# Convolutions one turn further ahead, in one stretch with the gate and the lora products

## The chip, the cores and the metric

The kernel runs on one core of a Trainium2 chip, as one launch. The metric is the device time of that core in microseconds (us). A number of runs is taken of each kernel and the median is compared; one more execution is recorded by the hardware profiler, and that is where the lines of this document come from.

## The reference

128 samples of 64 channels by 1024 positions pass through two residual layers, all in float32.

```
h   = gelu(cond @ W0 + b0); h = gelu(h @ W1 + b1)
att = softmax(h @ W2 + b2)                       # 8 weights per sample
y0  = (att-mixed 64x64 matrix of the sample) @ x + att @ bias_k
x   = x + (y0 @ B) @ A.T + ffn_bias              # rank 128, layer 0
y   = grouped conv(x, 9 taps, 4 groups) + context(cond) + fside
x   = x + y @ W_up.T + lora(y)                   # layer 1, W_up 1024 x 1024
lora(y): one of 4 experts by argmax(y @ gate_w.T + expert_bias), rank 8
```

## The kernel before

Two samples of 64 channels make a *pair* of 128 rows by 1024 columns; there are 64 pairs. Layer 1 works on two pairs at a time, so the main loop has 32 turns, d = 0 to 31. `manual_schedule` makes each engine run its instructions in the order in which the program emits them, and the order is written out by hand; nothing is reordered by a planner. A tile is handed on when its last reader is done, and tiles of one tag rotate through a fixed number of buffers. The tag "bank" has 4 PSUM banks, used in turn by almost everything; pb0 to pb3 are 4 further banks for the layer 1 products. x has 8 buffers, xt 3, yt 2, the convolution's input X 3.

*Layer 0 of a pair* is `layer0_in` (xt times B, L330, then a copy on ScalarE), `layer0_mix` (the mixing matrix, L340, then z on VectorE, or on ScalarE for the first four pairs) and `layer0_out` (z times AT, L361; VectorE adds it to x, L362). `layer0_out` then writes x to a DRAM tile x1d and reads it back in another arrangement as X, both from SyncE's DMA queue (L363, L368, L369). The mixing matrices of the first four pairs are built on the core (`own_bd`); those of the others are computed for all samples at once by `agg_all`, written to DRAM (`agg_out`) and read back in groups of two pairs by `load_cond`, with their bias rows (`load_rows`, "ab") and context rows ("cx").

*The convolution of a pair* has 9 taps over columns that are interleaved, so that even and odd columns share part of the work. `shared_in` multiplies X by the summed taps (L400), `shared_out` adds the context on VectorE (L415) and copies halves across partitions on ScalarE (L418). `differences` makes differences of neighbouring columns on GpSimd (L392, L393). `conv_in` multiplies those by the taps (L438), once for each sample, and `conv_out` adds the shared part on VectorE (L450), which gives y in the tile yt. Pairs 0 and 1 use a plain form (L429). The matmuls of L400, L429, L438 and of the gate (L496) use 64 of the array's columns each and go by twos to the two halves of the output's partitions; the profile shows them as 128\*64. Those of lora (L573) use 32 rows each and go by fours (32\*128). All others are 128\*128.

*Layer 1 of two pairs* multiplies 256 rows of y by W_up by a scheme with seven half-size products instead of eight: `ffn_sums` makes four sums of y on GpSimd (s0 to s3, L485 to L488), and `w_sum` makes combinations of W_up's quarters once at the start (T1, T2, T3, -T4 from w11, w12, w21, w22, on VectorE). `ffn_a` is the first product (and ScalarE's copy v of it, L479); `ffn` holds the others (all L465), u2 and u3 on VectorE (L556, L560), their adds to x on GpSimd (L561 to L563), the gate (`gate_in` L496, a copy zg on ScalarE, `gate` L511 and a chain of small VectorE instructions), the turn of the masked lora inputs (L536), the four lora products (L573) and the final adds to x on VectorE (L575), after which SyncE writes the two pairs out.

In turn d, TensorE does: the second product of d; gate and shared sum of pair 2d+2; T2, gate's fold, T3, T1, the last two products; lora; taps of 2d+2 and shared sum of 2d+3; layer 0 in of pairs 2d+4 and 2d+5; taps of 2d+3; the rest of layer 0 around the first product of d+1. Pairs are so convolved in the turn before they are used. GpSimd's queue holds, in a turn: the four sums, differences, two adds of the layer 0 bias (`add_fbias`, L581), the u adds, differences, and the loads of two pairs (`load_x`, xt L108 and x L109), where each load waits for a free buffer.

Of the kernel before, what the change touches and what calls it, by code (L numbers as in the profile page):

```python
# [41 lines left out]
P = 128  # L42
# [15 lines left out]
N = 512  # L58
# [10 lines left out]
def block(ctx: ExitStack, tc: tile.TileContext, a: dict, out: bass.AP):  # L69
# [65 lines left out]
        eng.dma_start(W[name], a[f"w{name}"])  # L135

    def load_w12(eng):
        for h in range(2):
            W12.append(tmp.tile([P, HC // 2, N], F32, tag=f"tmp{h}", name=f"w12_{h}"))
            eng.dma_start(W12[h], a["w12"][:, h * HC // 2 : (h + 1) * HC // 2])  # L140

    def w_sum(name, x, y):
        W[name] = const.tile([P, HC, N], F32, name=f"w{name}")
        if "12" not in (x, y):
            nc.vector.tensor_tensor(W[name], W[x], W[y], ALU.subtract)
            return
        for h in range(2):
            part = slice(h * HC // 2, (h + 1) * HC // 2)
            u, w = (W12[h] if n == "12" else W[n][:, part] for n in (x, y))
            nc.vector.tensor_tensor(W[name][:, part], u, w, ALU.subtract)  # L150


    X = []
# [24 lines left out]
    def load_cond(g):  # L178

        if g * GP >= FIRST:  # L180
            bds[g] = BD[g % NBD]
            for b in range(2):
                nc.sync.dma_start(
                    bds[g].rearrange("(r two) t b o -> two r t b o", two=2)[b, :, :, b, :],
                    aggd.rearrange("(t two) r o -> two r t o", two=2)[b, :, g * GP : (g + 1) * GP],
                )
            load_rows(g, aggbs, aggbd, "ab")
        load_rows(g, ctxs, ctxd, "cx")

    def load_rows(g, tiles, src, tag):  # L190
# [107 lines left out]

    def agg_all():

        first = ytp.tile([NB, 4, 512], F32, tag="yt", name="agg0")
        second = [xpool.tile([NB, 2, 512], F32, tag="x", name=f"agg1{j}") for j in range(2)]
        to = aggd.rearrange("b i o -> b (i o)").rearrange("b (j h n) -> h b j n", j=4, h=2)
        aggs.extend([(to[0], first), (to[1][:, :2], second[0]), (to[1][:, 2:], second[1])])
        for h in range(2):
            ps4 = [spare(j, f"pagg{h}_{j}") for j in range(4)]
            for j in range(4):
                rows = slice(32 * j, 32 * (j + 1))
                nc.tensor.matmul(ps4[j], attT[rows, :], wa[rows, h], start=True, stop=True)
            for j in range(4):  # L310
                to = second[j // 2][:, j % 2] if h else first[:, j]
                if j % 2:
                    nc.scalar.copy(to, ps4[j])
                else:
                    nc.vector.tensor_copy(to, ps4[j])
            yield

    def agg_out():
# [1 line left out]
            nc.sync.dma_start(to, agg)  # L320


    xbs, z0s, yts, opened = {}, {}, {}, {}
    diffs, pms, m2s, pcs = {}, {}, {}, {}

    def layer0_in(pr):
        xt = xts.pop(pr)
# [146 lines left out]
    def ffn_a(d):  # L474

        opened[d] = [psb.tile([P, N], F32, tag=f"pb{i}", name=f"pb{i}_{d}") for i in range(4)]
        product(opened[d][0], halves(d)[0][0], W["11"])
        v = sums.tile([P, N], F32, tag="v", name=f"v{d}")
        nc.scalar.copy(v, opened[d][0])  # L479
        return v  # L480

    def ffn_sums(d):
        (a0, a1), (b0, b1) = halves(d)
        s = [sums.tile([P, HC, P], F32, tag=f"s{i}", name=f"s{i}_{d}") for i in range(4)]
        nc.gpsimd.tensor_tensor(s[0], b0, b1, ALU.add)  # L485
        nc.gpsimd.tensor_tensor(s[1], s[0], a0, ALU.subtract)  # L486
        nc.gpsimd.tensor_tensor(s[2], a0, b0, ALU.subtract)
        nc.gpsimd.tensor_tensor(s[3], a1, s[1], ALU.subtract)  # L488
        return s

    def gate_in(d):
        yt = yts[d]
        pg = bank(f"pg{d}")
        for c in range(NC):
            rows = slice(c % 2 * GT, (c % 2 + 1) * GT)
            nc.tensor.matmul(  # L496
                pg[rows, : 2 * P].rearrange("m (t r) -> m t r", t=2),
                gl[:, c, :],
                yt[:, :, c],
                start=c < 2,  # L500
                stop=c >= NC - 2,
            )
        zg = sp.tile([P, 2, P], F32, tag="zg", name=f"zg{d}")
        nc.scalar.copy(zg.rearrange("p t r -> p (t r)"), pg[:, : 2 * P])
        return zg

    def gate(d, zg):

        pt = bank(f"pgt{d}")
        for t in range(2):  # L510
            nc.tensor.matmul(pt[:, t * GL : (t + 1) * GL], zg[:, t], fold, start=True, stop=True)  # L511
# [26 lines left out]
        nc.scalar.copy(zt, p[:, :P])  # L538
        return zt

    def ffn(d, v, s, then=None):
        (a0, a1), (b0, b1) = halves(d)
        p = opened.pop(d)
        xa, xb = xs.pop(2 * d), xs.pop(2 * d + 1)
        lo, hi = slice(0, N), slice(N, L)
        if d:
            product(p[0], a1, W["21"], False)
        zg = gate_in(d)
        if 2 * d + 2 < NPAIR:
            shared_in(2 * d + 2)  # L550
            shared_out(2 * d + 2)
        if then:
            then()
        product(p[1], s[1], W["T2"])
        u2 = sums.tile([P, N], F32, tag="u2", name=f"u2_{d}")
        nc.vector.tensor_tensor(u2, p[1], v, ALU.add)  # L556
        zm = gate(d, zg)
        product(p[2], s[2], W["T3"])
        u3 = sums.tile([P, N], F32, tag="u3", name=f"u3_{d}")
        nc.vector.tensor_tensor(u3, p[2], u2, ALU.add)  # L560
        nc.gpsimd.tensor_tensor(xa[:, hi], xa[:, hi], u2, ALU.add)  # L561
        nc.gpsimd.tensor_tensor(xb[:, lo], xb[:, lo], u2, ALU.add)
        nc.gpsimd.tensor_tensor(xb[:, hi], xb[:, hi], u3, ALU.add)  # L563
        product(p[3], s[0], W["T1"])
        zt = turn(d, zm)
        nc.vector.tensor_tensor(xb[:, hi], p[3], xb[:, hi], ALU.add)
        product(p[2], b1, W["-T4"], False)
        product(p[3], s[3], W["22"], False)
        del yts[d]
        last = bank(f"pl{d}")  # L570
        for j, to in enumerate((p[0], p[3], p[2], last)):
            rows = slice(j * ER, (j + 1) * ER)
            nc.tensor.matmul(to, zt[rows, :], lb[rows, :], start=j == 3, stop=True, skip_group_check=j < 3)  # L573
        for x, cols, part in ((xa, lo, p[0]), (xa, hi, p[3]), (xb, lo, p[2]), (xb, hi, last)):
            nc.vector.tensor_tensor(x[:, cols], part, x[:, cols], ALU.add)  # L575
            if part is p[3]:
                nc.sync.dma_start(out[2 * d], xa)
        nc.sync.dma_start(out[2 * d + 1], xb)

    def add_fbias(pr, eng):  # L580
# [4 lines left out]
        layer0_mix(pr)  # L585
        layer0_out(pr)

    def between(d, A, B, a, b):

        ahead = A < NPAIR  # L590
        conv_in(a, 0)
        conv_in(a, 1)
        shared_in(b)
        conv_out(a, 0)
        conv_out(a, 1)
        if ahead:
            layer0_in(A)
        shared_out(b)
        if ahead:
            layer0_in(B)  # L600
            layer0_mix(A)
        conv_in(b, 0)
        conv_in(b, 1)
        conv_out(b, 0)
        conv_out(b, 1)
        if ahead:
            layer0_out(A)
            layer0_mix(B)
        v = ffn_a(d)
        if ahead:  # L610
            layer0_out(B)
        return v


    condition()
# [15 lines left out]
    add_fbias(0, nc.vector)  # L631
    own_bd(1)
    layer0_mix(0)
    load_w("11", nc.scalar)
    b_column()
    agg_b_all()
    own_bias(1)
    load_cond(0)
    layer0_out(0)

    load_w12(nc.sync)
    add_fbias(1, nc.vector)
    add_fbias(2, nc.gpsimd)
    layer0_in(1)
# [2 lines left out]
    layer0_mix(1)  # L647
    own_att(2)
    own_att(3)
    load_cond(1)  # L650
    layer0_out(1, lambda: load_w("22", nc.sync))
    load_w("21", nc.sync)
    load_x(3, nc.sync)
    gl = loaded("gl", [P, NC, GT])
    lb = loaded("lb", [P, N])
    add_fbias(3, nc.gpsimd)
    wsum = const.tile([P, NGC, P], F32, tag="sel", name="wsum")
    nc.gpsimd.tensor_tensor(wsum, ws[:, :, 0], ws[:, :, 1], ALU.add)  # L658
    next(agg)
    own_bd(2)  # L660
    own_bias(2)
    layer0_in(2)
    conv(0)
    layer0_mix(2)
    layer0_out(2)
    w_sum("T1", "12", "11")
    own_bd(3)
    own_bias(3)
    v = ffn_a(0)
    conv(1)  # L670
    load_x(4)
    load_x(5)
    layer0_in(3)
    w_sum("T2", "22", "T1")
    w_sum("T3", "22", "12")
    product(opened[0][0], halves(0)[0][1], W["21"], False)
    layer0_mix(3)
    w_sum("-T4", "21", "T2")

    agg_out()  # L680
    for d in range(NPAIR // 2):
        pairs = [pr for pr in (2 * d + 4, 2 * d + 5) if pr < NPAIR]
        more = 2 * d + 2 < NPAIR
        s = ffn_sums(d)
        if more:
            differences(2 * d + 2)
        if pairs:
            load_cond(d + 2)
        for pr in pairs:
            add_fbias(pr, nc.gpsimd)  # L690
        ffn(d, v, s, None if d else lambda: layer0_out(3))
        if more:
            differences(2 * d + 3)
        for pr in (2 * d + 6, 2 * d + 7):
            if pr < NPAIR:
                load_x(pr)
        if more:
            v = between(d + 1, 2 * d + 4, 2 * d + 5, 2 * d + 2, 2 * d + 3)


def _by_rows(v):
# [101 lines left out]
```

## Time and profile before

| | us |
|---|---|
| median of 6 runs | 1357.84 (1356.05 to 1358.95) |
| the profiled execution | 1356.28 |
| its span, first to last instruction | 1354.5 |
| TensorE matmuls busy | 1336.6 |
| VectorE (DVE) busy | 588.2 |
| GpSimd (POOL) busy | 617.9 |
| ScalarE (ACT) busy | 142.2 |
| mean granted TensorE clock | 0.997 |
| one turn of the loop (697.85 to 738.97) | 41.12 |

PE is TensorE's matmuls, PEld its weight loads, SP is SyncE, whose queue issues most DMAs. L12 is line 12 of the kernel. In a timeline row stand: start, time from start to end of the merged group, engine, line, operation, output and inputs by the program's names, rows and columns of the array in use, shape, number of instructions, and in brackets the idle time before and what ended it. A float32 matmul shows as two instructions. Matmuls are pipelined and their ends are modelled, so groups overlap in the rows; distances between starts are what they take.

### The profile page before, as it was taken

The numbers are of one execution on the slowest core, as the hardware profiler recorded it, in microseconds if no ns is written. First come the engines' busy times: TensorE is split into PE (matmuls) and PEld (weight loads), VectorE is DVE, ScalarE is ACT, GpSimd is POOL, SyncE is SP. The second block draws the span as 40 slices with busy tenths as digits, with TensorE's granted clock in tenths as the row PEclk, the third lists the DMA queues.
The fourth block names the chain that finished last, engine by engine and source line by source line (L and its number), as shares of the span: only waits on it lengthen the run. The fifth ranks groups of instructions, "written<-read, shape, count | busy, mean of one in ns | idle before, by whom it ended". The sixth has DMA issues, their size and how long they took to land.

```text
span 1354.5 us, 18285 instructions
## 1 busy us (share of the span) xinstructions
PE 1336.6 (99%) x7303; PEld 757.9 (56%) x7303; DVE 588.2 (43%) x980; ACT 142.2 (10%) x310; POOL 617.9 (46%) x549
## 2 busy tenths in 40 slices
PE   8899999999999999999999999999999999999997
PEld 6555555555555555455555555555555554555553
DVE  5744334344344344344443343443443443444442
ACT  2101101101011011011011011010110110110100
POOL 1554455434554444554444554345544445544322
PEclk9999999999999999999999999999999999999999
DMA  8963344543444534445444445434445344454220
GB/s 294 300 187 128 119 134 135 166 137 123 121 139 144 158 127 128 115 135 166 144 131 119 135 135 166 136 124 120 139 144 159 126 129 115 134 166 146 67 79 31
DMA packets 184004, 189.37 MB, mean 140 GB/s; under 512 B 17392, under 2 KB 156656, under 8 KB 183536
## 3 DMA queue, kind: packets, MB, share of 16 engines
q1 hardware_dynamic: 165632, 121.09, 31.6%
q0 software_dynamic: 17280, 62.92, 13.2%
q10 hardware_dynamic: 1008, 4.19, 0.8%
q8 instruction: 58, 0.95, 0.3%
q14 instruction: 26, 0.21, 0.1%
HBM read 118.90 MB, written 69.27 MB: 139 GB/s over the span
## 4 chain that ended last, share of the span: by engine, by line
PE 95%; issue 2%; DMA 1%; POOL 1%; SPq 0%; DVE 0%; DVEq 0%; ACT 0%; POOLq 0%; ACTq 0%
PE pb L465 57%; PE pc L438 9%; PE pxb L330 8%; PE pd L361 8%; PE pg L496 4%; PE pm L400 4%; PE pb L573 2%; DMA x<-in_x 1%; PE pz L340 1%; PE pgt L511 1%; POOL x L581 0%; PE pzt L536 0%; POOL s L485 0%; POOL wsum L658 0%; POOL s L486 0%
## 5 line engine op out<-in xcount | busy, mean ns | idle before, releaser
L465 PE MATMUL pb<-wT,s 128*128 128x512 f32 x768 | 346.0, 600 | 2.3 <-POOL s L486 2.3
L465 PEld LDWEIGHTS pb<-wT,s 128*128 128x128 f32 x768 | 140.8, 190 | 161.7 <-issue 158.2
L465 PE MATMUL pb<-w,yt 128*128 128x512 f32 x512 | 230.4, 593 | 0.7 <-ACT v L479 0.7
L108 POOL DMA_DIRECT2D xt<-in_xt x60 | 33.2, 553 | 321.8 <-PE pxb L330 321.8
L581 POOL TENSOR_TENSOR x<-x,ffn_bias 128x1024 f32<-128x1024 f32 x62 | 146.0, 2375 | 44.0 <-DMA x<-in_x 44.0
L575 DVE TENSOR_TENSOR x<-pb,x 128x512 f32<-128x512 f32 x96 | 60.3, 684 | 231.5 <-PE pl L573 231.5
L415 DVE TENSOR_TENSOR m<-pm,cx 64x512 f32<-64x512 f32 x124 | 85.1, 686 | 167.0 <-PE pm L400 165.1
L465 PEld LDWEIGHTS pb<-w,yt 128*128 128x128 f32 x512 | 94.7, 190 | 108.4 <-issue 106.7
L362 DVE TENSOR_TENSOR x<-pd,x 128x512 f32<-128x512 f32 x128 | 88.2, 689 | 119.4 <-PE pd L361 119.3
L450 DVE TENSOR_TENSOR yt<-pc,m 128x512 f32<-128x512 f32 x124 | 124.8, 1086 | 22.6 <-PE pc L438 22.6
L361 PE MATMUL pd<-AT,z 128*128 128x512 f32 x256 | 124.1, 606 | 0.9 <-DVE attx L261 0.5
L330 PE MATMUL pxb<-B,xt 128*128 128x128 f32 x1024 | 124.8, 280 | 0.0
L438 PEld LDWEIGHTS pc<-ws,df 128*64 128x64 f32 x1984 | 107.0, 137 | 27.3 <-issue 23.5
L330 PEld LDWEIGHTS pxb<-B,xt 128*128 128x128 f32 x1024 | 118.6, 194 | 6.5 <-DVE x L575 5.1
L438 PE MATMUL pc<-ws,df 128*64 128x128 f32 x1984 | 122.0, 276 | 0.0
L465 PE MATMUL pb<-w-T,yt 128*128 128x512 f32 x256 | 115.3, 593 | 0.2 <-DVE u L560 0.2
L465 PE MATMUL pb<-w,s 128*128 128x512 f32 x256 | 115.1, 592 | 0.0
L485 POOL TENSOR_TENSOR s<-yt 128x512 f32<-128x512 f32 x32 | 42.5, 1328 | 145.7 <-DVE yt L450 145.7
L392 POOL TENSOR_TENSOR df<-X 128x512 f32<-128x512 f32 x62 | 64.4, 1039 | 88.4 <-DMA X<-x1d 85.9
L465 PEld LDWEIGHTS pb<-w,s 128*128 128x128 f32 x256 | 48.6, 190 | 61.2 <-issue 61.2
L418 ACT COPY m<-m 64x512 f32<-64x512 f32 x124 | 76.5, 617 | 58.6 <-DVE m L415 55.2
L465 PEld LDWEIGHTS pb<-w-T,yt 128*128 128x128 f32 x256 | 46.1, 190 | 55.2 <-issue 54.8
(110 smaller groups left out, 1157.8 us busy)
## 6 DMA issues: line engine op xcount, KB each, us to landing
x1d<-x SPq DMA_DIRECT2D x128, 256.0 KB, 2.2
X<-x1d SPq DMA_DIRECT2D x128, 256.0 KB, 3.8
out<-x SPq DMA_DIRECT2D x64, 512.0 KB, 2.6
xt<-in_xt POOLq DMA_DIRECT2D x60, 512.0 KB, 3.8
x<-in_x POOLq DMA_DIRECT2D x60, 512.0 KB, 4.6
cx<-ctxd SPq DMA_DIRECT2D x32, 128.0 KB, 3.5
ab<-aggbd SPq DMA_DIRECT2D x30, 128.0 KB, 3.3
w<-in_w SPq DMA_DIRECT2D x2, 1024.0 KB, 9.0
```

What stands on the lines that cost most here:

```text
L330: nc.tensor.matmul(pxb[:, :P], xt[:, c, :], bt[:, c, :], start=(c == 0), stop=(c == NC - 1))
L361: nc.tensor.matmul(pd, z0, at[:, cols], start=True, stop=True)
L362: nc.vector.tensor_tensor(x[:, cols], pd, x[:, cols], ALU.add)
L392: nc.gpsimd.tensor_tensor(diffs[pr][:, :, 0], at_even, at_odd, ALU.subtract)
L400: nc.tensor.matmul(pm[b * H : (b + 1) * H, g * P : (g + 1) * P], blocks(pr, b, g, 1), wsum[:, g], start=True, stop=True,)
L415: nc.vector.tensor_tensor(by_group(m2[half, b]), by_group(pm[half]), context(pr, b, half), ALU.add)
L418: nc.scalar.copy(m2[other, b], m2[half, b])
L438: nc.tensor.matmul(pc[o * H : (o + 1) * H, cols], diffs[pr][:, 2 * g + b, o], ws[:, g, o], start=True, stop=True,)
L450: nc.vector.tensor_tensor(yt.rearrange("m q (o g two) -> m two g q o", two=2, g=NGC)[:, b], by_group(pcs.pop((pr, b))), context(pr, b) if ...
L465: nc.tensor.matmul(to, yt[:, c], w[:, c], start=first and c == 0, stop=c == HC - 1, skip_group_check=not first)
L575: nc.vector.tensor_tensor(x[:, cols], part, x[:, cols], ALU.add)
L581: eng.tensor_tensor(xs[pr], xs[pr], fbias, ALU.add)
```

## The change

In turn d, the convolutions of pairs 2d+4 and 2d+5 are done instead of those of 2d+2 and 2d+3, and all of both stands in one place, after layer 1's products of turn d: both shared sums, the gate's input product of turn d+1, the four groups of taps, then lora of turn d (`tiles`). Their evictions on VectorE are put in between, and the final adds of turn d (`results`) come after them. The gate's fold and its chain (`gate`) come ahead of T2. The sums of y for turn d+1 are emitted ahead of that turn, behind the loads of pairs 2d+8 and 2d+9, which are one turn further ahead too, as are the loads of mixing matrices; context rows are loaded by a function of their own, `load_context`. Ahead of the loop, two more pairs are convolved and two more pass through layer 0. Therefore the start is in another order: w11 is loaded by SyncE, behind pair 1, instead of by ScalarE; gl and lb by ScalarE; pairs 3 and 4 earlier by SyncE; w12 in four parts in the slots of s0 to s3; and the aggregates wait in the slots of T3 and -T4 until they are written out, ahead of the reading of X3.

```diff
     def load_w12(eng):
-        for h in range(2):
-            W12.append(tmp.tile([P, HC // 2, N], F32, tag=f"tmp{h}", name=f"w12_{h}"))
+        for c in range(HC):
+            W12.append(sums.tile([P, N], F32, tag=f"s{c}", name=f"w12_{c}"))
...
     def agg_all():
-        first = ytp.tile([NB, 4, 512], F32, tag="yt", name="agg0")
-        second = [xpool.tile([NB, 2, 512], F32, tag="x", name=f"agg1{j}") for j in range(2)]
+            agg = const.tile([NB, 4, 512], F32, tag=("wT3", "w-T4")[h], name=f"agg{h}")
...
+    def ffn(d):
+        zm = gate(d)
         product(p[1], s[1], W["T2"])
         u2 = sums.tile([P, N], F32, tag="u2", name=f"u2_{d}")
         nc.vector.tensor_tensor(u2, p[1], v, ALU.add)
-        zm = gate(d, zg)
+        nc.gpsimd.tensor_tensor(xa[:, hi], xa[:, hi], u2, ALU.add)
+        nc.gpsimd.tensor_tensor(xb[:, lo], xb[:, lo], u2, ALU.add)
+        if 2 * d + 4 < NPAIR:
+            differences(2 * d + 4)
         product(p[2], s[2], W["T3"])
         u3 = sums.tile([P, N], F32, tag="u3", name=f"u3_{d}")
         nc.vector.tensor_tensor(u3, p[2], u2, ALU.add)
         nc.gpsimd.tensor_tensor(xb[:, hi], xb[:, hi], u3, ALU.add)
+        if 2 * d + 5 < NPAIR:
+            differences(2 * d + 5)
         product(p[3], s[0], W["T1"])
+        nc.vector.tensor_tensor(xb[:, hi], p[3], xb[:, hi], ALU.add)
         zt = turn(d, zm)
         product(p[2], b1, W["-T4"], False)
         product(p[3], s[3], W["22"], False)
...
+    def tiles(d, zt, a, b):
+        if a < NPAIR:
+            shared_in(a)
+            shared_in(b)
+        if d + 1 < NPAIR // 2:
+            pg = gate_in(d + 1)
+        if a < NPAIR:
+            conv_in(a, 0)
+            shared_out(a)
+            conv_in(a, 1)
+            shared_out(b)
+            conv_in(b, 0)
+        if d + 1 < NPAIR // 2:
+            gate_out(d + 1, pg)
+        if a < NPAIR:
+            conv_in(b, 1)
+            conv_out(a, 0)
+        lora(d, zt)
+        if a < NPAIR:
+            conv_out(a, 1)
+            conv_out(b, 0)
+            conv_out(b, 1)
+        results(d)
...
-    load_w("11", nc.scalar)
...
     layer0_out(0)
-    load_w12(nc.sync)
+    load_x(3, nc.sync)
...
-    layer0_out(1, lambda: load_w("22", nc.sync))
+    gl = loaded("gl", [P, NC, GT], eng=nc.scalar)
+    lb = loaded("lb", [P, N], eng=nc.scalar)
+    layer0_out(1)
+    load_w("11", nc.sync)
     load_w("21", nc.sync)
...
     layer0_in(2)
     conv(0)
     layer0_mix(2)
-    layer0_out(2)
-    w_sum("T1", "12", "11")
+    layer0_out(2, lambda: load_x(4, nc.sync))
     own_bd(3)
     own_bias(3)
+    load_w12(nc.sync)
+    load_w("22", nc.sync)
+    layer0_in(3)
     conv(1)
+    layer0_mix(3)
+    layer0_out(3, agg_out)
+    add_fbias(4, nc.gpsimd)
+    differences(2)
+    gate_out(0, gate_in(0))
+    ffn_a(0)
+    w_sum("T1", "12", "11")
+    w_sum("T2", "22", "T1")
     load_x(5)
+    load_cond(2)
+    layer0_in(4)
+    differences(3)
+    ffn_second(0)
+    shared_in(2)
+    shared_in(3)
+    conv_in(2, 0)
...
+    conv_out(3, 1)
+    add_fbias(5, nc.gpsimd)
+    layer0_in(5)
+    layer0_mix(4)
     w_sum("T3", "22", "12")
     w_sum("-T4", "21", "T2")
-    agg_out()
+    ffn_sums(0)
+    layer0_mix(5)
+    layer0_out(4)
+    load_x(6)
+    load_x(7)
     for d in range(NPAIR // 2):
+        more = d + 1 < NPAIR // 2
+        ahead = [pr for pr in (2 * d + 6, 2 * d + 7) if pr < NPAIR]
+        if 2 * d + 5 < NPAIR:
+            layer0_out(2 * d + 5)
+            load_context(d + 2)
+        if ahead:
+            load_cond(d + 3)
+        for pr in ahead:
+            add_fbias(pr, nc.gpsimd)
+        tiles(d, ffn(d), 2 * d + 4, 2 * d + 5)
+        for pr in (2 * d + 8, 2 * d + 9):
             if pr < NPAIR:
                 load_x(pr)
         if more:
+            ffn_sums(d + 1)
+        for pr in ahead:
+            layer0_in(pr)
+        if ahead:
+            layer0_mix(ahead[0])
+        if more:
+            ffn_a(d + 1)
+        if ahead:
+            layer0_out(ahead[0])
+            layer0_mix(ahead[1])
+        if more:
+            ffn_second(d + 1)
```

## The prediction

> **What bounds the kernel now.** I read the page first, by engine and by chain.
>
> ```profile
> PE 1336.6 (99%) x7303; PEld 757.9 (56%) x7303; DVE 588.2 (43%) x980; ACT 142.2 (10%) x310; POOL 617.9 (46%) x549
> ...
> PE 95%; issue 2%; DMA 1%; POOL 1%; SPq 0%; DVE 0%; DVEq 0%; ACT 0%; POOLq 0%; ACTq 0%
> ```
>
> TensorE is the path; DVE and POOL are under half busy. So only time inside the TensorE stream can be won, and only a new wait of TensorE can lose. A busy PE may still lose time between matmuls, so I read one turn of the loop in PE's timeline (start, busy time, line, shapes, count).
>
> ```profile
> 697.85 1.97 PE L438 MATMUL pc<-ws,df 128*64 128x128 f32 x32
> 699.64 1.04 PE L400 MATMUL pm<-wsum,X 128*64 128x128 f32 x16
> 700.62 3.84 PE L330 MATMUL pxb<-B,xt 128*128 128x128 f32 x32
> ...
> 704.61 1.97 PE L438 MATMUL pc<-ws,df 128*64 128x128 f32 x32
> 706.50 1.98 PE L361 MATMUL pd<-AT,z 128*128 128x512 f32 x4
> ...
> 708.55 3.60 PE L465 MATMUL pb<-w,yt 128*128 128x512 f32 x8
> 711.98 1.88 PE L361 MATMUL pd<-AT,z 128*128 128x512 f32 x4
> 713.70 3.60 PE L465 MATMUL pb<-w,yt 128*128 128x512 f32 x8
> 717.23 1.95 PE L496 MATMUL pg<-yt,gl 128*64 128x256 f32 x16
> 719.00 1.04 PE L400 MATMUL pm<-wsum,X 128*64 128x128 f32 x16
> 719.98 3.70 PE L465 MATMUL pb<-wT,s 128*128 128x512 f32 x8
> ```
>
> No row has a wait, and a turn lasts 41.12 (the next L438 starts at 738.97). But the distance from start to start depends on the neighbour's shape (128\*64 is half the columns, 128\*128 the full array). Eight L465 take 3.43 before a full-array neighbour (708.55 to 711.98) and 3.53 before a tile one (713.70 to 717.23): 0.10 on the way in. Four L361 take 1.72 (711.98 to 713.70) but 1.83 after tiles (706.50 to 708.33): 0.11. 32 L438 take 1.79 when more tiles follow (697.85 to 699.64) and 1.89 when the full array follows (704.61): 0.10 on the way out; and against twice an L400 group without its way out (0.88) the first takes 0.04 at the start. A trip into tiles and back costs 0.35; the trace's starts in ns give 0.093 + 0.051 + 0.098 + 0.103 = 0.345.
>
> **Removing trips.** In before, each turn makes three trips: gate and first shared sum; lora, first pair's taps, second shared sum; second pair's taps. That is 3 in turns 0 to 29, 2 in turns 30 and 31 each, and 2 for the opening's convolutions: 96. After has one per turn (32) and four in the opening (convolutions 0 and 1, the first gate, pairs 2 and 3): 36. 60 x 0.345 = **-20.7 us**. Taps move to the other side of lora: "tiles to 32 rows" and "32 rows to full" replace "full to 32 rows" and "32 rows to tiles". The first isn't in this trace; from the nearest switches it costs 0 to 0.2, I take 0.10, like tiles to full, and then the two orders are equal; the bound is 0.1 x 31 = 3 us either way.
>
> The Trainium skill ("TensorEngine Tiling (Array Packing)", Key Properties) says that changing the tiling mode drains the array, and that another tile of the same mode does not; it gives no time, and the rows above are that price. Its section PSUM Bottleneck speaks against this change: tiling speeds up TensorE, but not the reading of PSUM, which may become the bottleneck. That is weighed next, from rows.
>
> **Does the long stretch stall?** From its first matmul: shared sums end at 0.9 and 1.8, the gate (1.73) at 3.5, four tap groups of 0.87 at 4.4, 5.3, 6.2 and 7.0, lora (1.07) at 8.2. DVE must do four L415 (0.69), four L450 (1.09) and four L575 (0.63), 9.6 in all, from 1.1 on. Four banks rotate: the second tap group needs the first shared sum read (2.6; wanted 4.4), the third the second one (3.9; 5.3), the fourth the gate's copy, which on ACT stands behind four m copies of 0.62 (4.9; 6.2), and lora's last bank the first L450 (5.7; 7.1). The smallest margin is 1.1. DVE ends at about 11.5, but between lora and the next product stand L330 and L340, to 12.2, and that product needs only the first L575 (9.6). So nothing, in turns that have L330.
>
> **Where that cover is gone.** Turns 29 and 30 have no layer 0 left to do. In turn 29 the product waits for the first L575: 1.3, and the second product follows the first at once and waits for v's copy on ACT: 0.7 (before has that once, 0.73, in its last turn). In turn 30: 0.9. **+2.9 us**.
>
> **POOL and SP.** Sums (four of 1.26) and bias adds (4.69 for two) are as many as before; a load goes one turn earlier, and eight x buffers now mean that load 2d+8 waits until output 2d has landed. The sums stand behind these loads: first x complete at 10.2, output 2.6 later (page, median landing), then second x, two waits and four issues of 0.55: sums from 14.7, the one that T2 needs at 17.3. T2 starts at 23.1: 5.8 to spare. The row and context loads change their place on SP, which is mostly idle in a turn: nothing. Gate ahead of T2 instead of behind it: the same 0.36.
>
> **The opening is dearer.** It now has pairs 2 and 3 convolved and layer 0 of pairs 4 and 5 done before the first T2 (61.55 in before). DMA limits here: 271 GB/s at 91% share from 25 to 62, against 136 in the loop turn. In SP's timeline:
>
> ```profile
> 39.83 1.80 SPq L363 DMA_DIRECT2D x1d<-x  x2
> 51.23 0.52 SPq L368 DMA_DIRECT2D X<-x1d  x1
> ```
>
> X waits 11 for a 0.5 MB write behind about 3 MB of loads. In after, the same queue holds, ahead of X3: X0, x3, X1, w11, w21, x4, X2, w12, w22, both aggregates (2 MB), four x1d writes, and x5 and the gate's weights beside it. From 20 us that is some 14 MB: at 285 GB/s (the mean of 20 to 50) it lands at 70, at 340 at 62. I take 63, since the queue is rarely empty in after, and full stretches ran at 330 to 407 (20 to 25, 60 to 65). When does PE want it? X0 no longer shares with w11 (moved off ACT's queue) and comes at 28.0, so these two waits shrink:
>
> ```profile
> 30.59 5.12 PE L429 MATMUL pc<-ws,X 128*64 128x128 f32 x64 [2.75 <-DMA X<-x1d]
> ...
> 43.28 3.72 PE L429 MATMUL pc<-ws,X 128*64 128x128 f32 x64 [0.90 <-DMA X<-x1d]
> ```
>
> From 28.0 by the rows' lengths: convolution 0 3.65, mix with z's wait 1.3, out 1.8; layer 0 of pair 3 1.85, convolution 1 3.65, mix 1.3, out 1.8; gate 1.9, product 3.5, L330 1.85, product 3.5, one shared sum 0.9: shared sum 3 is due at 55. Wait 8.
>
> The first of these also shows the clock: after the wait of 2.75 it ran 1.40 longer than the second; the granted clock was 0.64 in 31 to 34.5. So the wait for X3 costs some more at a slow clock: 1.4 by this row, up to twice that after a longer wait; I take 1.7, near the row. By the skill's "TensorE: Matmul & The Clock Gate" (Part 1) an idle window of about 3.4 us halves the clock for about as long; an estimate from that is 1.7 as well.
>
> Then DVE. X3 at 63, shared sum and taps 4.4, slow clock 1.7: taps end at 69. L330, pz and z of pair 4 to 71.8; T3 (2.4, as T1 took at 39.59), T4 (3.4, as at 55.68 beside POOL's sums), and only then z of pair 5: 77.9. PE wants it at 73.2: wait 4.7. T2 starts at 80.1. Last, POOL: sums after T3 (which reads w12 in their slots), 3.25 for the first beside T4 as at 56.90, to 81.2; x7 issued 82.9, landing 4.6; two bias adds to 91.1, two u adds (1.26 each), the differences put among them (two of 1.04), third u add, then DVE's read of p[3] to 97.7. The turn's last product wants it at 94.0 (80.1 and four products): wait 3.7. Waits of after: 0.5 + 0.4 (X0) + 0.4 + 0.4 (z) + 8 + 1.7 + 4.7 + 3.7 = 19.8. Before, over the same work: 0.5 + 2.75 + 1.4 + 0.4 + 0.9 + 1.3 + 2.3 + 0.2 = 9.8. **+10 us**; ends: 0 (no extra wait at all) and +20 (X3 at 70 and 3 more in the chain).
>
> Edits with no price of their own: w12 in four loads and T1 and T3 in quarters instead of halves (same elements), the aggregates in the slots of T3 and -T4 (read out by 62, before T3 at 71.8), x3 earlier on SP and x4 on SP instead of POOL (counted in the queue above).
>
> **Sum.** -20.7 + 2.9 + 10 = **-7.8**. The profiled execution took 1356.28 (span 1354.5, 1.8 around it), 1.56 under the median; I apply the difference to the median: 1357.84 - 7.8 = **1350.0 us**. Its own range, with the opening's ends and lora's 3, the ends of both being unlikely together: 1338 to 1358. About 0.2%, 2.7 us, is what a measurement can tell from no change.
>
> **Rivals.**
> *The opening costs nothing extra*: X3 comes by 57 and the DVE chain is shorter. For it: some loads of before only stood behind SP's own waits, DMA being 7% busy in 50 to 52.5. Against: more bytes are now due by then. 1357.84 - 20.7 + 2.9 = 1340. Chance 0.15.
>
> *POOL sets the turn (slower)*: output lands late, so POOL's load holds the sums, and T2 waits in every turn. It decides when the landing takes over 2.6 + 5.8 = 8.4; 1 us past that is 30 us: 1380. At 0.3 us a turn the gain is gone. For it: x loads in the opening took 8.9. Against: median 2.6, DMA share 46% in the turn. Chance 0.08.
>
> *The trips aren't saved*: the wait at a switch is only uncovered weight loading that comes back inside the longer stretch. 1350.0 + 20.7 = 1371. Against: tile groups of different lines follow each other at their inner pace (L496 to L400). Chance 0.04.
>
> *The opening eats it all*: 1355 to 1359. Chance 0.07. The forecast keeps 0.66.
>
> Faster: 0.66 + 0.15, less a little at the forecast's upper end, 0.80; same 0.07; slower 0.13. The range 1338 to 1358 leaves out POOL, the trips and some of the ends.
>
> **What would show it.** Right: a turn of 40.4 with no PE wait; L438, L400, L496 and L573 in one block of 8.2; a PE wait for X of 5 to 14 us near 55; a wait on z near 75; one product waiting on L575 in turns 29 and 30. Wrong: a PE wait on POOL sums in steady turns, a turn still of 41.1, or X3 before 58.

## The result and the profile after

The changed kernel takes 1359.33 us (median of 20 runs) beside 1357.54 of before (40 runs): a ratio of 1.0015, 95% interval 1.0009 to 1.0021. That is a small loss, 1.8 us, where 7.8 us of gain were forecast, and it lies 1.3 us above the stated range. The profiled execution took 1360.25 with a span of 1358.4, 3.9 more than before.

The page of after first, the same two lines as of before:

```profile
PE 1320.6 (97%) x7303; PEld 761.3 (56%) x7303; DVE 554.5 (41%) x984; ACT 139.0 (10%) x310; POOL 614.8 (45%) x547
...
PE 92%; DMA 5%; DVE 2%; POOL 0%; issue 0%; ACT 0%; SPq 0%; DVEq 0%; ACTq 0%; POOLq 0%
```

TensorE is busy 16.0 less with the same 7303 instructions, and yet the span is longer: the chain now holds 5% DMA (1% in before) and 2% VectorE (0%). Line numbers move with the edits: in after, the gate's fold is L514, lora L580, the final adds to x L586 and the bias adds L591. One turn in PE's timeline of after:

```profile
702.41 0.53 PE L514 MATMUL pgt<-fold,zg 128*128 128x36 f32 x4
...
720.23 1.97 PE L400 MATMUL pm<-wsum,X 128*64 128x128 f32 x32
722.03 1.90 PE L496 MATMUL pg<-yt,gl 128*64 128x256 f32 x16
723.75 3.67 PE L438 MATMUL pc<-ws,df 128*64 128x128 f32 x64
727.35 0.70 PE L580 MATMUL pb<-lb,zt 32*128 32x512 f32 x3
...
728.42 3.84 PE L330 MATMUL pxb<-B,xt 128*128 128x128 f32 x32
...
742.85 0.53 PE L514 MATMUL pgt<-fold,zg 128*128 128x36 f32 x4
```

The tiles stand in one block, 720.23 to 728.42, 8.2 long. No row has a wait. From fold to fold it is 40.44, against 41.12 in before; 41.12 less two trips of 0.345 is 40.43. So the loop does what was forecast, to a hundredth. The loss is in the opening. PE's waits, longest first (reason, total, times, longest), and the rows around them:

```profile
PE pm L400 <- DMA X<-x1d: 12.4, 1, 12.4
PE pd L361 <- DVE z L348: 6.1, 1, 6.1
PE pb L465 <- DVE x L567: 3.1, 1, 3.1
PE pb L465 <- DVE x L586: 1.7, 2, 0.9
PE pc L429 <- DMA X<-x1d: 1.7, 1, 1.7
PE pb L465 <- ACT v L479: 1.4, 2, 0.7
```

```profile
56.50 1.10 PE L400 MATMUL pm<-wsum,X 128*64 128x128 f32 x16
70.04 1.98 PE L400 MATMUL pm<-wsum,X 128*64 128x128 f32 x16 [12.44 <-DMA X<-x1d]
71.77 4.83 PE L438 MATMUL pc<-ws,df 128*64 128x128 f32 x64
76.53 2.05 PE L330 MATMUL pxb<-B,xt 128*128 128x128 f32 x16
...
79.31 1.92 PE L361 MATMUL pd<-AT,z 128*128 128x512 f32 x4
87.31 3.78 PE L361 MATMUL pd<-AT,z 128*128 128x512 f32 x4 [6.09 <-DVE z L348]
...
108.54 5.24 PE L465 MATMUL pb<-w,s 128*128 128x512 f32 x8 [3.05 <-DVE x L567]
...
136.69 10.55 PE L465 MATMUL pb<-wT,s 128*128 128x512 f32 x24
```

X3 is X, the convolution's input, of pair 3. L567 is VectorE's read of p[3], the bank that the last product of a turn wants next. The last row is T2 of turn 1.

Behind each of the three waits a row is longer than its twin: four L361 take 3.78 beside 1.92, the eight L465 take 5.24 beside 3.60, and 64 L438 take 4.83 beside 3.67 in the turn. The granted clock by stretches (stretch, length, PE busy and its instructions, granted clock, DMA share, GB/s) says why:

```profile
70.00:75.00 5.00, 4.96 (x55) 0.59 0.18 36
75.00:80.00 5.00, 4.81 (x52) 1.00 0.00 0
...
88.00:92.00 4.00, 4.00 (x10) 0.60 0.75 188
108.00:112.00 4.00, 3.46 (x5) 0.57 0.37 79
```

After each of these waits the clock stays at half for some time into the work. The lateness of X3 is seen in SP's timeline (start of the issue, its length):

```profile
45.90 0.52 SPq L368 DMA_DIRECT2D X<-x1d  x1
...
47.17 2.03 SPq L140 DMA_DIRECT2D w<-in_w  x4
49.24 0.43 SPq L135 DMA_DIRECT2D w<-in_w  x1
50.61 1.41 SPq L363 DMA_DIRECT2D x1d<-x  x2
53.19 1.07 SPq L319 DMA_DIRECT2D aggbd<-aggb  x1
54.36 1.47 SPq L319 DMA_DIRECT2D aggd<-agg  x2
58.81 0.56 SPq L368 DMA_DIRECT2D X<-x1d  x1
59.52 1.69 SPq L369 DMA_DIRECT2D X<-x1d  x1
```

X2 can be asked for only at 45.90, when its x1d has landed; w12 and w22 follow it in the queue, and the two halves of the write of pair 3, issued from 50.61, land behind them at 58.8 and 59.5. X3 is asked for then, behind the 2 MB of aggregates, and its second half lands at 69.9.

### The profile page after: what moved, and what is told of

It reads as the page before. It is cut to its first block, busy times and chain, and to the rows that moved or that the text cites. A ratio compares the mean times of both kernels' runs of the same rounds, so it can differ in the third digit from the quotient of the medians.

```text
span 1358.4 us, 18275 instructions
## 1 busy us (share of the span) xinstructions
PE 1320.6 (97%) x7303; PEld 761.3 (56%) x7303; DVE 554.5 (41%) x984; ACT 139.0 (10%) x310; POOL 614.8 (45%) x547
## 3 DMA queue, kind: packets, MB, share of 16 engines
q10 hardware_dynamic: 1152, 3.67, 0.8%
## 4 chain that ended last, share of the span: by engine, by line
PE 92%; DMA 5%; DVE 2%; POOL 0%; issue 0%; ACT 0%; SPq 0%; DVEq 0%; ACTq 0%; POOLq 0%
PE pb L465 56%; PE pxb L330 8%; PE pc L438 8%; PE pd L361 7%; PE pm L400 4%; PE pg L496 4%; PE pb L580 2%; DMA x1d<-x 2%; DMA X<-x1d 1%; PE pz L340 1%; PE pgt L514 1%; DMA x<-in_x 1%; DMA xt<-in_xt 0%; PE pc L429 0%; PE pzt L539 0%
## 5 line engine op out<-in xcount | busy, mean ns | idle before, releaser
L465 PE MATMUL pb<-wT,s 128*128 128x512 f32 x768 | 337.5, 596 | 0.0
L109 POOL DMA_DIRECT2D x<-in_x x59 | 31.1, 528 | 504.8 <-DVE z L348 419.3
L465 PEld LDWEIGHTS pb<-wT,s 128*128 128x128 f32 x768 | 143.5, 190 | 168.4 <-issue 168.1
L465 PE MATMUL pb<-w,yt 128*128 128x512 f32 x512 | 230.8, 593 | 3.1 <-DVE x L586 1.7
L591 POOL TENSOR_TENSOR x<-x,ffn_bias 128x1024 f32<-128x1024 f32 x62 | 144.7, 2353 | 48.0 <-DMA x<-in_x 48.0
L465 PEld LDWEIGHTS pb<-w,yt 128*128 128x128 f32 x512 | 92.4, 190 | 98.6 <-issue 92.2
L330 PEld LDWEIGHTS pxb<-B,xt 128*128 128x128 f32 x1024 | 118.9, 194 | 24.4 <-DVE yt L450 22.0
L361 PE MATMUL pd<-AT,z 128*128 128x512 f32 x256 | 122.9, 602 | 7.7 <-DVE z L348 6.1
L450 DVE TENSOR_TENSOR yt<-pc,m 128x512 f32<-128x512 f32 x124 | 121.4, 1098 | 21.2 <-ACT m L418 20.8
L330 PE MATMUL pxb<-B,xt 128*128 128x128 f32 x1024 | 124.9, 280 | 0.0
L465 PE MATMUL pb<-w,s 128*128 128x512 f32 x256 | 116.7, 599 | 3.1 <-DVE x L567 3.1
L465 PE MATMUL pb<-w-T,yt 128*128 128x512 f32 x256 | 115.2, 592 | 0.0
L438 PE MATMUL pc<-ws,df 128*64 128x128 f32 x1984 | 114.7, 274 | 0.0
L438 PEld LDWEIGHTS pc<-ws,df 128*64 128x64 f32 x1984 | 111.7, 138 | 4.3
L556 POOL TENSOR_TENSOR x<-x,u 128x512 f32<-128x512 f32 x32 | 40.4, 1264 | 140.2 <-DVE u L555 137.2
L361 PEld LDWEIGHTS pd<-AT,z 128*128 128x128 f32 x256 | 48.6, 192 | 68.3 <-issue 58.4
L465 PEld LDWEIGHTS pb<-w,s 128*128 128x128 f32 x256 | 49.2, 193 | 65.5 <-issue 61.6
L465 PEld LDWEIGHTS pb<-w-T,yt 128*128 128x128 f32 x256 | 46.1, 190 | 55.1 <-issue 55.1
L400 PEld LDWEIGHTS pm<-wsum,X 128*64 128x64 f32 x992 | 54.4, 140 | 36.2 <-issue 35.4
```

What stands on the lines that cost most here:

```text
L330: nc.tensor.matmul(pxb[:, :P], xt[:, c, :], bt[:, c, :], start=(c == 0), stop=(c == NC - 1))
L361: nc.tensor.matmul(pd, z0, at[:, cols], start=True, stop=True)
L400: nc.tensor.matmul(pm[b * H : (b + 1) * H, g * P : (g + 1) * P], blocks(pr, b, g, 1), wsum[:, g], start=True, stop=True,)
L438: nc.tensor.matmul(pc[o * H : (o + 1) * H, cols], diffs[pr][:, 2 * g + b, o], ws[:, g, o], start=True, stop=True,)
L450: nc.vector.tensor_tensor(yt.rearrange("m q (o g two) -> m two g q o", two=2, g=NGC)[:, b], by_group(pcs.pop((pr, b))), context(pr, b) if ...
L465: nc.tensor.matmul(to, yt[:, c], w[:, c], start=first and c == 0, stop=c == HC - 1, skip_group_check=not first)
```

## The experiments

Two theories stood against each other. *The opening*: a trip into tiles is worth 0.345 wherever it is, the loop keeps all of it, and all that is missing against the forecast are waits in the opening, one behind the other, and the slow clock behind them. *The loop*: the trips are worth less than counted, or their gain comes back elsewhere. Medians below stand beside 1359.33 of after; ratios are to before, measured on the same chip. Before took 1357.13 to 1357.71 on these chips (1357.54 beside after), so a few tenths of a microsecond between medians of different chips say nothing.

**A trip back.** The second pair's taps leave the stretch:

```diff
 def tiles(d, zt, a, b):
...
-            conv_in(b, 0)
...
-            conv_in(b, 1)
...
-            conv_out(b, 0)
-            conv_out(b, 1)
...
         for pr in ahead:
             layer0_in(pr)
+        if 2 * d + 5 < NPAIR:
+            for b in range(2):
+                conv_in(2 * d + 5, b)
+            for b in range(2):
+                conv_out(2 * d + 5, b)
```

> The change with the second pair's taps moved out of the stretch, behind the next pairs' L330: one more trip into tiles in 29 turns. Theory (a trip costs 0.345): a turn of 40.78 instead of 40.44 and 10 us more than the change, 1369. Rival (a switch is only uncovered weight loading, which the neighbours hide): turn and time as in the change, 1359.

1369.26 us, ratio 1.0090 (1.0076 to 1.0103): 9.9 more than after. PE's timeline of this run, from L330 to L330:

```profile
690.33 3.84 PE L330 MATMUL pxb<-B,xt 128*128 128x128 f32 x32
694.10 1.97 PE L438 MATMUL pc<-ws,df 128*64 128x128 f32 x32
...
731.11 3.84 PE L330 MATMUL pxb<-B,xt 128*128 128x128 f32 x32
```

A turn of 40.78, again without a wait. That is 0.34 more, and 29 trips of 0.345 are 10.0. The price of a trip holds, and the rival falls.

**The opening of before.** The opening and turn 0 are taken over from before; at the end of turn 0 the lead is built up, and the loop starts with turn 1:

```diff
...   (the opening of before, then turn 0 in before's order, without differences(4), (5))
     layer0_out(5)
+    ffn_sums(1)
+    load_cond(3)
...
+    ffn_second(1)
+    layer0_in(6)
+    layer0_in(7)
+    layer0_mix(6)
+    shared_in(4)
+    shared_in(5)
+    pg = gate_in(1)
+    conv_in(4, 0)
...
+    conv_out(5, 1)
+    layer0_out(6)
+    layer0_mix(7)
-    for d in range(NPAIR // 2):
+    for d in range(1, NPAIR // 2):
```

> The opening and turn 0 as in the kernel before; the longer lead (pairs 4 and 5 convolved, layer 0 of 6 and 7 done) is built up at the end of turn 0, and from turn 1 on the loop is that of the change. Theory (all that was lost against the forecast lies in the opening): T2 of turn 1 starts at 115 to 117 us instead of 136.6, turns stay at 40.44, time 1338 to 1341. Rival (the loop's gain is given back somewhere else, the opening does not matter): 1355 to 1359.

1341.56 us, ratio 0.9886 (0.9873 to 0.9900). In the runs with this opening most line numbers are 3 higher (L468 is after's L465). In PE's timeline T2 of turn 0 and of turn 1:

```profile
62.64 12.26 PE L468 MATMUL pb<-wT,s 128*128 128x512 f32 x24 [2.73 <-POOL s L488]
...
119.85 10.55 PE L468 MATMUL pb<-wT,s 128*128 128x512 f32 x24
```

T2 of turn 1 comes at 119.85, later than expected, but 16.8 sooner than in after (136.69); the median is 17.8 lower. The turns are the same in both. This settles the main question: with the opening of before the change gives 16 us against before, although waits of 3.17, 2.90 and 2.73 are left in that opening, and nothing is given back in the loop.

**The clock alone.** The wait for X3 is filled with idle products:

```diff
     shared_in(2)
+    busy(opened[0][1], 54)
     shared_in(3)
```

> The change with 54 products of the identity with itself, some 12 us, put on TensorE in front of the shared sum that waits for X3. Theory (the taps behind that wait are slow because the clock is taken back in it): X3 as late as before, but shared sum 3 and the taps of pairs 2 and 3 take 4.4 instead of 6.5, and all behind is 2 earlier: 1357. Rival (they are slow for another reason, such as the reads of X): still 6.5, time 1359 or more.

1357.68 us, ratio 1.0002 (0.9993 to 1.0010). PE's timeline:

```profile
58.04 12.32 PE L213 MATMUL pb<-ident 128*128 128x128 f32 x108
70.30 1.10 PE L400 MATMUL pm<-wsum,X 128*64 128x128 f32 x16
71.22 3.66 PE L438 MATMUL pc<-ws,df 128*64 128x128 f32 x64
74.82 2.05 PE L330 MATMUL pxb<-B,xt 128*128 128x128 f32 x16
```

Shared sum 3 and the taps take 4.52 (70.30 to 74.82) instead of 6.49 (70.04 to 76.53). So the slow clock costs 2.0 behind this wait, and its cause is the idle array, not the reads of X. X3 was there 1.0 sooner than in after (GpSimd starts to read it at 69.00, not 70.04), but TensorE was busy until 70.30, so that is not what made the taps faster. The trace's clock records agree: no half clock between 14.7 and 83.0 in this run, where after has 0.50 from 70.0 to 73.4.

**X3 ahead of the aggregates.**

```diff
-    layer0_out(3, agg_out)
+    layer0_out(3)
+    agg_out()
```

> The change with the aggregates written out behind the reading of X3 instead of ahead of it. Theory (X3 is late because of the bytes queued ahead of it): X3 lands at 63 to 66 instead of 70, the wait in front of shared sum 3 falls from 12.4 to 6 to 9, time 1354 to 1356. Rival (the wait moves on to the mixing matrices of pairs 4 and 5, read back from the aggregates): a new wait at L340 of pair 4, time 1359.

1355.72 us, ratio 0.9994 (0.9984 to 1.0005): 3.6 less than after by the medians, though the 11 runs spread from 1353.52 to 1360.21. PE's timeline:

```profile
65.59 1.98 PE L400 MATMUL pm<-wsum,X 128*64 128x128 f32 x16 [8.20 <-DMA X<-x1d]
...
75.74 1.98 PE L361 MATMUL pd<-AT,z 128*128 128x512 f32 x4 [1.25 <-DVE z L348]
83.81 3.78 PE L361 MATMUL pd<-AT,z 128*128 128x512 f32 x4 [6.08 <-DVE z L348]
```

X3 comes 4.5 sooner; so much of its lateness are the 2 MB ahead of it. 8.2 remain, and the rival is right in part, by a new wait of 1.25 at z of pair 4: VectorE waits 2.31 for the bias rows "ab" of that pair, which are read back behind the aggregates (issued at 71.93, landed at 75.25). The wait on z of pair 5 stands unchanged.

**z of pair 5 ahead of T3.**

```diff
     layer0_mix(4)
+    layer0_mix(5)
     w_sum("T3", "22", "12")
     w_sum("-T4", "21", "T2")
     ffn_sums(0)
-    layer0_mix(5)
```

> The change with z of pair 5 emitted ahead of T3 and -T4 on VectorE. Theory (the three waits of the opening stand one behind the other, and the last is set by GpSimd's own chain: sums, loads, X4, bias adds, u adds): the wait on z goes, T2 waits for its sum instead and starts at 87 to 88 (91.4 in the change), but the last product of turn 0 still starts at about 108, so its wait grows from 3.1 to 6 or more: 1357.5 to 1359.5. Rival (each wait costs its own time): 6 to 8 us less, 1352.

1360.40 us, ratio 1.0017 (1.0007 to 1.0027): nothing gained. PE's timeline:

```profile
88.18 1.07 PE L514 MATMUL pgt<-fold,zg 128*128 128x36 f32 x4 [5.39 <-DVE x L362]
89.06 13.39 PE L465 MATMUL pb<-wT,s 128*128 128x512 f32 x24
...
108.86 5.17 PE L465 MATMUL pb<-w,s 128*128 128x512 f32 x8 [2.88 <-DVE x L567]
```

The wait on z is gone, but the fold waits 5.39 for VectorE's adds to x, which now stand behind T3 and -T4 and hold its bank. T2 gains 2.3 (89.06), less than expected, and the last product starts where it did: GpSimd's chain decides there. That its wait did not grow to 6 as expected is the slow clock's doing: T2, T3 and T1 took 13.39 instead of 10.55, with half clock from 88.0 to 94.8.

**Late bias adds.** In turn 0, GpSimd does the u adds before the bias adds of pairs 6 and 7 and the differences of pair 4:

```diff
-        if 2 * d + 4 < NPAIR:
+        if d and 2 * d + 4 < NPAIR:
             differences(2 * d + 4)
...
+        if not d:
+            differences(4)
...
-        for pr in ahead:
-            add_fbias(pr, nc.gpsimd)
-        tiles(d, ffn(d), 2 * d + 4, 2 * d + 5)
+        if d:
+            for pr in ahead:
+                add_fbias(pr, nc.gpsimd)
+        zt = ffn(d)
+        if not d:
+            for pr in ahead:
+                add_fbias(pr, nc.gpsimd)
+        tiles(d, zt, 2 * d + 4, 2 * d + 5)
```

> The change with the bias adds of pairs 6 and 7 and the differences of pair 4 moved behind the u adds in turn 0, on GpSimd. Theory (the last product of turn 0 waits because VectorE's read of p[3] waits for the third u add, which stands behind these): that wait of 3.1 and the slow clock after it (1.6) go: 1354 to 1355. Rival (the wait moves on to the taps of pair 4 or 5, whose differences are now late): a wait in front of L438 of turn 0, 1358 or more.

1355.37 us, ratio 0.9983 (0.9975 to 0.9992): 4.0 less than after. The last product starts without a wait and runs at full clock:

```profile
105.81 3.60 PE L465 MATMUL pb<-w,s 128*128 128x512 f32 x8
```

3.05 of wait and 1.64 of slow clock came from one order of GpSimd's queue. The taps of pair 4 and 5 did not wait.

**All three together** (the last three edits in one).

> The change with X3 ahead of the aggregates, z of pair 5 ahead of T3, and the bias adds of pairs 6 and 7 and differences of pair 4 late, together. Theory (waits in a row): T2 of turn 0 at 81 to 83 instead of 91.4, no wait of the last product, 13 us less than the change: 1345 to 1348. Rival (the bytes due before turn 0 set the end of the opening whatever the order): 1352 to 1356.

1351.80 us, ratio 0.9955 (0.9942 to 0.9967): 7.5 less than after. The theory misses by 4; the time lies 0.2 below the rival's range. PE's timeline:

```profile
66.63 1.98 PE L400 MATMUL pm<-wsum,X 128*64 128x128 f32 x16 [9.20 <-DMA X<-x1d]
...
85.13 1.07 PE L514 MATMUL pgt<-fold,zg 128*128 128x36 f32 x4 [4.98 <-DVE x L362]
86.00 12.64 PE L465 MATMUL pb<-wT,s 128*128 128x512 f32 x24
```

T2 starts at 86.0 and not at 82: the fold's wait, known from the run with z of pair 5 first, takes the place of z's. And 9.2 of wait for X3 are left with no aggregates ahead of it. This opening needs X3 before it may start turn 0, and X3 can be asked for only when its write has landed, at 59.5 here, behind w12 and w22; that these two loads are the reason is read from the queue, no run moves them alone. These three shuffles do not cure it; other work for TensorE in that time does, as in the opening of before.

**A tuned opening.** To the run with the opening of before, with sums 0 ahead of the bias add of pair 3 and the loads of pairs 4 and 5 on GpSimd, `load_cond(3)` ahead of the first product of turn 1, and layer 0 out of pair 6 ahead of the stretch of pairs 4 and 5:

```diff
-    add_fbias(3, nc.gpsimd)
     wsum = const.tile([P, NGC, P], F32, tag="sel", name="wsum")
...
+    ffn_sums(0)
+    add_fbias(3, nc.gpsimd)
     load_x(4)
     load_x(5)
...
     agg_out()
-    ffn_sums(0)
...
+    load_cond(3)
     ffn_a(1)
     layer0_out(5)
     ffn_sums(1)
-    load_cond(3)
...
     layer0_in(6)
-    layer0_in(7)
     layer0_mix(6)
+    layer0_in(7)
+    layer0_out(6)
+    layer0_mix(7)
     shared_in(4)
...
     conv_out(5, 1)
-    layer0_out(6)
-    layer0_mix(7)
```

> As the run with the opening of before, and the first sums ahead of the loads and bias adds on GpSimd, the mixing matrices of pairs 6 and 7 read earlier, and layer 0 out of pair 6 ahead of the stretch of pairs 4 and 5. Theory (what is left in that opening are waits of T2 for its sum, 2.7, of L340 for the matrices, 1.2, and of L361 for z, 0.8): these go, 1337 to 1339.5. Rival (they stand in front of a transfer that is late anyway, X2, X3 or X5): 1341.

1345.39 us, ratio 0.9908 (0.9895 to 0.9922): 3.8 more than without these edits, a miss of both theories. T2 does start at 60.97 without a wait, but behind it stands a new one:

```profile
79.46 6.53 PE L468 MATMUL pb<-w,s 128*128 128x512 f32 x8 [4.39 <-DVE x L570]
```

It is the known one, at L570 here: x4 and x5 are loaded later, GpSimd waits for them with the bias adds, and the u adds stand behind. So those two bias adds are moved behind the u adds as well:

```diff
-    add_fbias(4, nc.gpsimd)
-    add_fbias(5, nc.gpsimd)
...
-    lora(0, ffn(0))
+    zt = ffn(0)
+    add_fbias(4, nc.gpsimd)
+    add_fbias(5, nc.gpsimd)
+    lora(0, zt)
```

> As the tuned opening, with the bias adds of pairs 4 and 5 behind the u adds of turn 0. Theory (its loss against the plainer run was one wait on GpSimd's bias adds, 4.4, and 3.0 of slow clock behind it): both go, the last product of turn 0 starts at 75, time 1337 to 1339. Rival (the gains of that opening are taken by the next transfer in line): 1341 to 1343.

1336.51 us, ratio 0.9843 (0.9829 to 0.9858): the fastest of all, 20.8 below before and 22.8 below the change. PE's timeline:

```profile
60.04 10.55 PE L468 MATMUL pb<-wT,s 128*128 128x512 f32 x24
...
73.97 3.60 PE L468 MATMUL pb<-w,s 128*128 128x512 f32 x8
...
113.66 10.55 PE L468 MATMUL pb<-wT,s 128*128 128x512 f32 x24
```

No wait from 60 on in turn 0 but one of 0.4; T2 of turn 1 is 23.0 sooner than in after, and that is the whole difference of the medians.

**How near the stretch is to its limit.** The final adds of a turn go ahead of three evictions of taps:

```diff
         lora(d, zt)
+        results(d)
         if a < NPAIR:
             conv_out(a, 1)
             conv_out(b, 0)
             conv_out(b, 1)
-        results(d)
```

> The change with the final adds of a turn (four L586) ahead of the last three evictions of taps on VectorE, instead of behind them. Theory (the long stretch is free only because VectorE takes banks in the order in which TensorE wants them; L330 needs the bank of the second tap group): a wait of about 4 in front of L330 in each of 29 turns, 1460 to 1480. Rival (VectorE at 41% has room in any order): 1359.

1482.03 us, ratio 1.0915 (1.0897 to 1.0934). PE's timeline:

```profile
704.18 5.47 PE L330 MATMUL pxb<-B,xt 128*128 128x128 f32 x32 [2.56 <-DVE x L586]
...
748.87 5.47 PE L330 MATMUL pxb<-B,xt 128*128 128x128 f32 x32 [2.56 <-DVE x L586]
```

A turn of 44.69, 4.25 more, 29 times. The size is as expected, its parts are not: the wait is 2.56, and 1.63 are L330 at a slow clock (5.47 beside 3.84), which came in 28 of the 29 turns. Nor does L330 wait for the bank of the second tap group, as was expected: it starts at 748.87, right behind the last final add (748.81), while that group's eviction has only begun (748.73). Ahead of the final adds VectorE stands idle for 2.49, since they wait for lora. The order of VectorE's queue is so a condition under which the long stretch is free, at a VectorE busy share of 41% in after.

## Why the prediction was wrong

**Right: the trips.** Turn 40.44 as forecast, 0.68 less than 41.12, and the run with one trip more prices it by itself (9.9 for 29). The term of -20.7 stands. The lora switches, bounded at 3 us, cost what was assumed: 64 L438 take 3.60 ahead of lora (723.75 to 727.35) and 3.59 ahead of the full array (111.05 to 114.64 in the run with the opening of before), and lora takes 1.07 in before and in after. **Right: no stall in the loop**; no PE wait in a full turn, and the block of 8.2 left VectorE room, in the order in which it takes the banks. POOL did not set the turn: the sums start 14.7 after the block's first matmul (734.90 and 720.23), as worked out. **Right: the last turns**, waits of 0.91, 0.73, 0.77 and 0.68 where before had 0.73: +2.4, forecast +2.9.

**Wrong: the size of the opening.** This is the step that failed. The mechanism and the places were right (X3, then z of pair 5, then p[3]), but the term was +10 and measures +22: 3.9 of span are -20.7 + 2.4 + 22.2. That figure is a remainder; summed directly, from 20 us to the last product of turn 0 after has 25.6 of waits and 5.6 of slow clock, before 8.3 and 1.4 over the same work, which is +21.4. By its parts: the wait for X3 was 12.4, not 8, since it landed at 70 and I took 63 between the ends of 62 and 70, on the ground that the queue is rarely empty. The fast rate of 340 GB/s did hold from 35 to 65 (339), but 20 to 35 had only 227 and 65 to 70 only 164, and the mean from 20 to 70 was 288, the slow end. Of the lateness, 4.5 were the aggregates ahead of X3; the rest is read from SP's rows, where X2 and X3 each wait for a write that stands behind loads. X1, put at no wait, cost 1.65. The wait on z was 6.1, not 4.7: T3 took 4.6, not 2.4, beside GpSimd's sums. The 2.4 was T1's row; T3's own row in before, 5.59 at 50.17 with GpSimd at work, was not used. And I counted the slow clock once, at 1.7; it came three times, 2.0, 2.0 and 1.6, once behind each wait, 3.9 more. It was put at nothing behind z and p[3], though the waits forecast there, 4.7 and 3.7, were longer than the 2.75 on which the slow clock had been read. These make 4.4 + 1.7 + 1.4 + 3.9 = 11.4 of the 12.2 that are missing; the small terms cancel among themselves.

The rival "the opening eats it all" named 1355 to 1359 with a chance of 0.07; it was the case that came, a little beyond its end. The bound of +20 for the opening was a bound from the same queue model as the value; nothing in it allowed for the clock behind the second and third wait. And that bound by itself gives 1360, so the stated range, which ended at 1358, was narrower than the opening's own doubt.

## What to carry to other kernels

When a loop is bound by TensorE without a wait, the distances from start to start between groups of different shapes still show what their order costs: here 0.345 us for each trip from the full array into tiles and back, 60 times. A longer lead in a loop is paid in its opening, where more has to be loaded and done before the first turn; the lead can be built up inside the first turns instead, behind work that is already there, and this was worth 18 of the 23 us between the change and the best version. In a queue that is served in order, look for the one instruction that another engine needs and let nothing stand ahead of it that waits for a load: this was worth 4.0 us in one run and 8.9 in another.

## What the runs showed of the hardware

Waits of TensorE of 2 to 3.2 us were often, but not always, followed by half clock, and their length alone does not tell: it came behind 2.73 (opening of before), 3.05 (after), 2.05 (last run, turn 0) and 2.56 (28 of 29 turns of the last run, whose mean granted clock fell to 0.955), but not behind 1.68 (X3 first), 2.34 (before), 3.00 (the fastest run) or 2.90 and 3.17 (opening of before). The clock records show what does tell. They lie on a grid of 3.413 us: in after, half clock begins at 60.47, 84.36 and 108.25, which are 7 steps of 3.413 apart. Counted by these steps, in the twelve traces and from 13 us on, half clock followed each step of full clock in which TensorE had been idle for 1.95 us or more, and none in which it had been idle for 1.87 or less; in between, one went to half (1.90) and two did not (1.88, 1.91). So the wait of 3.00 in the fastest run, which the grid cuts into 1.67 and 1.34, cost only its own length, and the wait of 2.05, which fell into one step, cost 1.8 more. Where half clock came behind a wait of 2 to 3 us, the row behind it mostly took 1.4 to 1.8 longer. How the grid lies in the executions that were not profiled is not known.

The Trainium skill ("TensorE: Matmul & The Clock Gate", "Why this matters for your kernels") says to leave no idle gap over about 3 us between bursts; the runs here agree in kind, but a gap of 2.05 was enough, and one of 3.17 was not. The records of half clock inside the work lasted 3.4, 6.8, 10.2, 13.7 and 17.1 us, multiples of 3.413, and the page's window (Part 1) is 3.413 us.
